# A transformer layer with FP4 feed-forward on one core: separate scale buffers for the last tiles, and some layernorm and rotary work moved from VectorE to ScalarE and GpSimd

## The chip, the cores and the metric

The kernel runs on one core of a Trainium2 chip. The metric is the device time of one execution in microseconds (us); the time of a kernel is the median of its runs. The engines are named as in the profile: PE is TensorE (matrix products; PEld its weight loads), DVE is VectorE, ACT is ScalarE, POOL is GpSimd, SP is SyncE, which issues the transfers (SPq is its queue).

## The reference

The input x is 2 sequences of 2048 tokens with 256 features. The layer is, cut to what matters:

```python
def reference(x, Wq, bq, Wk, bk, Wv, bv, Wo, bo, w_gate, w_up, w_down):
    x = x + attention(layernorm(x))      # 16 heads of 16, causal softmax
    x = x + ffn(layernorm(x))
    return x

def layernorm(x, eps=1e-5):
    m, v = mean(x, -1), var(x, -1)
    return (x - m) / sqrt(v + eps)

def rope(Y):                             # on q and k, per head
    Y2 = concat([-Y[..., 8:], Y[..., :8]], -1)
    return Y * cos + Y2 * sin

def fp4_quant_dequant(x):                # blocks of 16 along the last axis
    scale = maximum(max(abs(x)) / 6, 1e-12)
    return nearest_fp4(x / scale) * scale

def fp4_linear(x, w):
    return fp4_quant_dequant(x) @ fp4_quant_dequant(w).T

def ffn(x):                              # 256 -> 704 -> 256
    h = silu(fp4_linear(x, w_gate)) * fp4_linear(x, w_up)
    return fp4_linear(h, w_down)
```

## The kernel before

**Tiling.** A chunk is 512 tokens of one sequence; there are eight, (0,0) to (0,3) and (1,0) to (1,3), in this order. A tile is 128 tokens; a chunk has four. The heads are handled in four groups of four for each chunk, which makes 32 slots.

**A chunk's way.** `norm_steps` loads the four tiles of x, takes mean and variance (`deviation`: two DVE instructions, lines 515 and 516, then two on POOL, lines 520 and 521, that leave 1/sqrt(v+eps) in `rstd`), normalizes in place (`normed`, DVE, line 530), and turns the tile with PE (line 739), with a copy by ACT (line 745). `project_steps` makes q and k for half of the heads (`blk` 0 or 1; `i` is 0 for q and 1 for k): the product `pj` (PE, line 808), the biased copy `qb` (ACT, line 821), the product with the cosines into `t1` (DVE, line 828, from the PSUM result and the bias), the swapped halves in `t2` (DVE shuffle, line 854), times the sines (POOL, line 860), the sum into `t1` (POOL, line 863), a rounded copy `high` (ACT, line 886) and the rest `low` (POOL, line 890). High and low parts go to DRAM (SP, line 900) and come back laid out for the heads (lines 911 and 924). The first half chunk of all, called `early`, goes another way, without DRAM. In the trace the tile names of t1 and t2 are cut to "t", and "cs" is the table of cosines and sines.

For each slot, a maxima stage (`max_steps`: scores on PE, line 1064, row maxima on DVE, line 1088) precedes a value stage (`value_steps`: scores again, lines 1196 and 1204, the exponential on ACT, line 1219, and the product with the values, line 1252). The feed-forward part (`ffn_steps`) takes a tile through the attention's output product (line 1488), the first residual (line 1502), a second layernorm, `fp4` rounding (lines 554 to 593), the gate and up products (line 1543), tanh and products (1569, 1572, 1577), another `fp4` over 704 columns, and the down product (line 1636) with the second residual (line 1645). The four tiles of the last chunk (`last`) keep their data in buffers of the attention, which are free by then; they are called "own" in the trace. The bias `bob` is added to their x0 on POOL (line 1472).

`fp4` makes a small tile of scales and one of their inverses with DVE (lines 554, 557 and 558), nudges the inverse on POOL (562), multiplies by it (565), finds the rounding step on DVE (581 and 584), adds and subtracts it (587 and 590) and multiplies by the scale (593). The four large operations are POOL's, except for the 704 columns of the last chunk's tiles, where DVE has them. The weights go through `fp4` too, in the first part of the run; PE turns them (line 656). The small tiles come from rings of two buffers, called sc16 (16 blocks, for the 256 columns) and sc44 (44 blocks, for the 704 columns), for all tiles alike.

**What sets the order.** All work is handed to a planner (`Plan`) as tasks with an engine, an estimated cost, what they read and write, and a due number. The planner simulates the engines, always takes the task that can start first, and among tasks that can start within 0.03 us of each other the one with the lowest due number. The order that it finds is each engine's program order. Four of its rules matter here:

- A buffer of a ring is given to the tasks in the order in which they were added, which is that of the due numbers of their steps; only the PSUM banks `ps` are given in any order.
- A task whose due number is more than AHEAD = 3 above the lowest one that is still open isn't considered.
- PE prefers tasks of the tiling it is in (whole array, score strips, value strips): another tiling counts as CHANGE = 0.07 later in the due number.
- Due numbers are counted in units of which the 32 slots and the tail take 81 (`place`; `end` is 80). The tiles of the next to last chunk, (1,2), are spread until 4 units behind the end, so that the last of them is left for the tail, beside the last chunk's tiles. The last chunk's steps start at 80.97 with small distances.

Of the kernel before, what the change touches and what calls it, by code (L numbers as in the profile page):

```python
# [68 lines left out]
CHANGE = 0.07  # L69
# [4 lines left out]
ISSUE = 0.46  # L74

# [18 lines left out]
ROOM.update(x0=1, xT=1, x1=2, xn=2, h=1, hrT=1, step=1, fdev=2, sc16=2, sc44=2)  # L94
# [34 lines left out]
class Plan:  # L129
# [3 lines left out]
    def __init__(self):  # L133
        self.tasks = []
        self.made = {}

# [40 lines left out]
    def ordered(self):  # L177
# [33 lines left out]
        while len(out) < len(self.tasks):  # L211
            while dues and dues[-1][1] in done:
                dues.pop()
            horizon = dues[-1][0] + AHEAD
# [84 lines left out]
def landing(kb):  # L299
    return 2.0 + kb / 250  # L300
# [3 lines left out]
def layer_kernel(  # L304
# [199 lines left out]
    def deviation(pool, kind, src, thing, due):  # L504

        got = []
        dev = Thing(kind)

        def stats():
            bufs = ROOM[kind]  # L510
            st = pool.tile([P, 6], F32, tag="stats", name="stats", bufs=bufs)
            got.append(pool.tile([P, 2], F32, tag="mv", name="mv", bufs=bufs))
            got.append(pool.tile([P, 1], F32, tag="ve", name="ve", bufs=bufs))
            got.append(pool.tile([P, 1], F32, tag="rstd", name="rstd", bufs=bufs))
            nc.vector.bn_stats(st, src())
            nc.vector.bn_aggr(got[0], st)

        def power():
            mv, ve, rstd = got
            nc.gpsimd.tensor_scalar(ve, mv[:, 1:2], LN_EPS, 1.0, ALU.add, ALU.mult)  # L520
            nc.gpsimd.tensor_tensor(rstd, ve, minus_half, ALU.pow)

        add(DVE, 0.55, stats, [thing], [dev], due)
        add(POOL, 0.8, power, [dev, fixed], [dev], due)
        return got, dev

    def normed(dst, src, got, things, due):
        def run():
            mv, _, rstd = got
            nc.vector.tensor_scalar(dst(), src(), mv[:, 0:1], rstd, ALU.subtract, ALU.mult)  # L530

        add(DVE, 0.33, run, *things, due)

    def fp4(src, thing, r, n, engine=POOL, step_of=None):
# [3 lines left out]
        small16 = Thing("sc16" if nb <= 16 else "sc44")  # L538
# [10 lines left out]
        def scaled(due):  # L549
            def sizes():  # L550
                scale = ffn.tile([P, nb], F32, tag=f"scale{n}", name="scale")[:r]
                inv = ffn.tile([P, nb], F32, tag=f"inv{n}", name="inv")[:r]
                st["scale"], st["inv"] = scale, inv
                nc.vector.tensor_reduce(  # L554
                    scale, blocks(src()), AX.X, ALU.max, apply_absolute_value=True
                )
                nc.vector.tensor_scalar(scale, scale, 1.0 / 6.0, 1e-12, ALU.mult, ALU.max)
                nc.vector.reciprocal(inv, scale)  # L558
# [143 lines left out]
    def norm_steps(b, c):  # L702
# [22 lines left out]
        def stats(i, due):  # L725
            st[i]["by"] = deviation(pre, "dev", lambda: st[i]["x"], st[i]["in"], due)

        def norm(i, due):
            own = st[i]
            got, dev = own["by"]  # L730
            normed(lambda: own["x"], lambda: own["x"], got, ([dev], [own["in"]]), due)
# [27 lines left out]
    def project_steps(b, c, blk):  # L759
# [31 lines left out]
        def product_of(i, due):  # L791
# [31 lines left out]
            def cosines():  # L823
                if early and i:
                    got["t1"] = room(i, "t1")
                else:
                    got["t1"] = pre.tile([P, CH], F32, tag="t1", name="t1")
                nc.vector.scalar_tensor_tensor(
                    got["t1"], got["pj"], bias, angles[b, c][:, 0, :], ALU.add, ALU.mult
                )  # L830
# [7 lines left out]
            add(DVE, 0.67, cosines, [ps, cs_[b, c], bias_], [t1], due)  # L838
# [584 lines left out]
    def ffn_steps(b, c, i, last=False):  # L1423
# [33 lines left out]
        def load(due):  # L1457
# [4 lines left out]
            add(SP, landing(128), run, [rows_[b, c]] if last else [], [things["x0"]], due)  # L1462
# [46 lines left out]
        def scaled(due):  # L1509
# [9 lines left out]
            def step_of():  # L1519
# [5 lines left out]
                lambda: st["xn"], things["xn"], P, E, step_of=step_of if last else None  # L1525
# [68 lines left out]
        def scaled_gated(due):  # L1594
            def step_of():
# [10 lines left out]
                step_of if last else None,  # L1606
            )
# [256 lines left out]
    for at, step in sorted(begun + main + side, key=lambda x: x[0]):  # L1864
        step(at)
    for t in plan.ordered():
# [64 lines left out]
```

## Time and profile before

| What | Value |
|---|---|
| median of 3 runs | 1390.26 us (1388.22 to 1392.69) |
| profiled execution, its own time | 1384.36 us |
| its span, first to last instruction | 1382.6 us |
| PE busy | 1307.6 us, 95% |
| DVE busy | 1106.0 us, 80% |
| ACT busy | 752.0 us, 54% |
| POOL busy | 538.4 us, 39% |
| mean granted clock of TensorE | 0.972 |

The profile is a page of one execution. A row of 40 digits cuts the span into 40 equal slices and gives the busy share of each in tenths; PEclk is the clock that TensorE was granted, in tenths of full speed. A row of the timeline has the start, the duration, the engine, the line of the kernel, the operation, what it writes and reads with its shape, and in brackets how long the engine had been idle before it and what ended that. The table by stage gives busy time per engine for a stretch of the span. Matmul ends are modelled, so that a PE that is busy all the time is not PE at its peak.

### The profile page before, as it was taken

What the parts mean: (1) busy time and instruction counts of PE and PEld (TensorE: products, weight loads), DVE (VectorE), ACT (ScalarE), POOL (GpSimd) and SP (SyncE); (2) the same over time, 40 slices, a digit from 0 to 9 for tenths busy, and PEclk for the clock granted to TensorE, in tenths of its full rate; (3) what the DMA queues carried; (4) which work ended last, traced back from release to release, by engine and by line L of the source; (5) the groups of instructions that cost most, each with busy time, mean ns of one, the idle gap of its engine ahead of it and who ended that gap; (6) DMA issues with size and microseconds to landing.
All of it is one profiled execution on the core that took longest, in us unless ns stands there. A gap on an engine that the chain in (4) does not pass through costs nothing.

```text
span 1382.6 us, 27442 instructions
## 1 busy us (share of the span) xinstructions
PE 1307.6 (95%) x10269; PEld 650.5 (47%) x10269; DVE 1106.0 (80%) x2415; ACT 752.0 (54%) x1670; POOL 538.4 (39%) x685
## 2 busy tenths in 40 slices
PE   6887999999999999999988999999999999999967
PEld 4444444444544444444454555454454444444445
DVE  7788989978889988875467978997879888884286
ACT  3532665556556566558643455455655566668711
POOL 4654735434323434314345544343443232311262
PEclk9976999999999999999999999999999999999989
DMA  2544433411221401211444414240130130000000
GB/s 88 132 130 103 100 89 66 102 35 55 56 46 39 109 22 35 67 32 51 98 107 108 104 30 107 65 97 18 55 82 20 43 81 9 9 6 5 13 9 19
DMA packets 61886, 84.37 MB, mean 61 GB/s; under 512 B 14772, under 2 KB 30520, under 8 KB 61752
## 3 DMA queue, kind: packets, MB, share of 16 engines
q1 hardware_dynamic: 61744, 82.61, 23.7%
q8 instruction: 81, 1.33, 0.4%
q14 instruction: 53, 0.43, 0.1%
q10 hardware_dynamic: 8, 0.00, 0.0%
HBM read 55.09 MB, written 27.49 MB: 60 GB/s over the span
## 4 chain that ended last, share of the span: by engine, by line
PE 62%; DVE 20%; POOL 5%; issue 5%; DMA 5%; ACT 2%; SPq 0%; POOLq 0%; DVEq 0%; ACTq 0%
PE av L1252 14%; DVE parts L1088 9%; PE sc L1064 9%; PE pg L1543 9%; PE sx L1196 8%; PE sx L1204 7%; PE pd L1636 5%; PE pj L808 3%; PE pth L1403 2%; PE po L1488 1%; PE pv L990 1%; DVE scale L554 1%; PE sc L1033 1%; DVE step L581 1%; DVE step L584 1%
## 5 line engine op out<-in xcount | busy, mean ns | idle before, releaser
L1219 ACT ACTIVATE ex<-sx 128x512 f32<-128x512 f32 (+3 forms) x1280 | 593.5, 538 | 345.8 <-PE sx L1204 207.9
L1088 DVE TENSOR_REDUCE parts<-sc 128x1 f32<-128x512 f32 (+3 forms) x1152 | 638.4, 611 | 64.8 <-PE sc L1064 49.2
L1204 PE MATMUL sx<-qT,kT 64*128 64x512 f32 (+3 forms) x1280 | 337.7, 523 | 0.0
L1064 PE MATMUL sc<-kT,qT 64*128 64x512 f32 (+3 forms) x1280 | 290.3, 432 | 12.5 <-DMA kT<-parts 4.2
L1252 PE MATMUL av<-ex,v 128*32 128x512 f32 (+3 forms) x2560 | 300.1, 541 | 0.0
L1196 PE MATMUL sx<-mT,less 64*128 64x512 bf16 (+3 forms) x1280 | 250.7, 356 | 9.3 <-DVE parts L1088 3.4
L1064 PEld LDWEIGHTS sc<-kT,qT 64*128 64x128 f32 x1280 | 139.1, 192 | 176.4 <-DVE parts L1088 55.2
L1196 PEld LDWEIGHTS <-less 64*128 64x128 bf16 x1280 | 68.5, 94 | 212.9 <-issue 205.4
L562 POOL TENSOR_SCALAR inv<-inv 128x16 f32<-128x16 f32 (+2 forms) x82 | 17.7, 216 | 384.8 <-DVE inv L558 362.9
L1204 PEld LDWEIGHTS sx<-qT,kT 64*128 64x128 f32 x1280 | 132.5, 196 | 13.0 <-issue 10.6
L1636 PE MATMUL pd<-wdT,hrT 128*128 128x256 f32 (+1 forms) x384 | 100.9, 402 | 2.0 <-ACT hrT L1407 1.4
L1252 PEld LDWEIGHTS av<-ex,v 128*32 128x32 f32 x2560 | 51.7, 108 | 69.8 <-issue 59.8
L860 POOL TENSOR_TENSOR t<-t,cs 128x512 f32<-128x512 f32 x31 | 39.9, 1287 | 106.7 <-DVE t L854 100.4
L1636 PEld LDWEIGHTS pd<-wdT,hrT 128*128 128x128 f32 (+1 forms) x384 | 68.1, 191 | 27.2 <-issue 13.6
L1088 DVE TENSOR_REDUCE mx<-sc 128x1 f32<-128x128 f32 (+3 forms) x128 | 54.6, 478 | 31.2 <-PE sc L1033 31.0
L808 PE MATMUL pj<-xnT,wqkT 128*128 128x512 f32 x128 | 75.3, 685 | 3.3 <-DVE v L999 1.7
L1543 PE MATMUL pg<-wgT,xT 128*128 128x352 f32 x224 | 77.3, 477 | 0.3 <-ACT xT L1407 0.2
L1543 PE MATMUL pg<-wuT,xT 128*128 128x352 f32 x224 | 74.5, 472 | 0.2
L1033 PE MATMUL sc<-pick,mask_q 64*128 64x64 bf16 x1024 | 71.8, 202 | 0.0
L587 POOL TENSOR_TENSOR h<-h,step 128x704 f32<-128x704 f32 x28 | 47.2, 1685 | 57.8 <-DVE step L584 54.5
L1033 PE MATMUL sx<-pick,mask_k 64*128 64x64 bf16 x1024 | 63.5, 197 | 0.0
L1569 ACT ACTIVATE h<-pg 128x352 f32<-128x352 f32 x64 | 29.9, 467 | 56.8 <-PE pg L1543 51.6
(156 smaller groups left out, 1522.3 us busy)
## 6 DMA issues: line engine op xcount, KB each, us to landing
qT<-parts SPq DMA_DIRECT2D x120, 128.0 KB
kT<-parts SPq DMA_DIRECT2D x120, 128.0 KB
parts<-high SPq DMA_DIRECT2D x30, 256.0 KB
parts<-t SPq DMA_DIRECT2D x30, 256.0 KB
sums<-avs SPq DMA_DIRECT2D x28, 256.0 KB
cs<-in_rope_dram SPq DMA_DIRECT2D x8, 512.0 KB
xin<-in_L_attn_x_dram SPq DMA_DIRECT2D x28, 128.0 KB
y<-sums SPq DMA_DIRECT2D x28, 128.0 KB
```

The source lines that it names most:

```text
L587: queue.tensor_tensor(src(), src(), st["step"], ALU.add)
L808: nc.tensor.matmul(got["pj"], lhsT=wqkT[:, k, i, cols], rhs=xnTs[b, c][:, k, :], start=(k == 0), stop=(k == KE - 1),)
L860: (nc.gpsimd if early and i == 0 else queue).tensor_tensor(swapped, swapped, angles[b, c][:, 1, :], ALU.mult)
L1033: nc.tensor.matmul(sc[h][:, col + at : col + at + STRIP], lhsT=strips(mask, h, half), rhs=strips(pick, h), start=False, stop=(half == 1),)
L1064: nc.tensor.matmul(sc[h][:, :cols], lhsT=strips(qT, h, d, slice(i * P, (i + 1) * P)), rhs=strips(kT, h, duo, slice(0, cols)), start=True, ...
L1088: nc.vector.tensor_reduce(dst, got[0][h][:, :cols], AX.X, ALU.max)
L1196: nc.tensor.matmul(sc[h][:, off:], lhsT=strips(less[d], h), rhs=strips(mT, h, slice(off, CH)), start=True, stop=False,)
L1204: nc.tensor.matmul(sc[h][:, off:], lhsT=strips(kT, h, duo, slice(jj, jj + P)), rhs=strips(qT, h, d, slice(off, CH)), start=False, stop=(j ...
L1219: nc.scalar.activation(st[j, d][:, h, off:], got[0][h][:, off:], AF.Exp, scale=HD**-0.5)
L1252: nc.tensor.matmul(st["av"][SLOT * s : SLOT * (s + 1), off:], lhsT=v[:, at : at + SLOT], rhs=st[j, d][:, h, off:], start=(j == 0), stop=(j ...
L1543: nc.tensor.matmul(got[half], lhsT=split("xrT")[:, k, :], rhs=wT[:, k, half * IH : (half + 1) * IH], start=(k == 0), stop=(k == KE - 1),)
L1636: nc.tensor.matmul(st["pd"], lhsT=st["hrT"][:n, k, :], rhs=wdT[:n, k, :], start=(k == 0), stop=(k == KI - 1),)
```

## The change

Five things are changed.

1. `deviation` and `normed` get `soon`, true for the chunks (0,0), (0,1) and (0,2) in `norm_steps`. POOL then makes a third small value, shift = -mean * rstd, and the layernorm is applied by ACT as rstd * x + shift, instead of by DVE.
2. For the same chunks, without the early half of (0,0), the cosines are multiplied by POOL, from the biased copy `qb`, instead of by DVE from the PSUM result.
3. The last chunk's tiles get rings of their own for the small scale tiles (endsc16 and endsc44, two buffers each).
4. The load of x0 for the last chunk's tiles no longer waits for the attention's rows, and its due number is 1.0 lower.
5. In the planner, CHANGE goes from 0.07 to 0.1, and once the lowest open due number has come to 72 (end - NEAR), tasks up to 50 units ahead are considered instead of 3.

```diff
-CHANGE = 0.07
+CHANGE = 0.1
...
+NEAR = 8.0
+
+SOON = ((0, 0), (0, 1), (0, 2))
+COS = SOON
...
+ROOM.update(..., sc16=2, sc44=2, endsc16=2, endsc44=2)
...
-            horizon = dues[-1][0] + AHEAD
+            horizon = dues[-1][0] + (AHEAD if dues[-1][0] < self.near_end else 50.0)
...
-    def deviation(pool, kind, src, thing, due):
+    def deviation(pool, kind, src, thing, due, soon=False):
...
+            if soon:
+                nc.gpsimd.tensor_scalar(shift, mv[:, 0:1], rstd, -1.0, ALU.mult, ALU.mult)
...
-        add(POOL, 0.8, power, [dev, fixed], [dev], due)
+        add(POOL, 0.8 + 0.22 * soon, power, [dev, fixed], [dev], due)
...
-    def normed(dst, src, got, things, due):
+    def normed(dst, src, got, things, due, soon=False):
...
+            if soon:
+                nc.scalar.activation(dst(), src(), AF.Identity, bias=shift, scale=rstd)
+            else:
+                nc.vector.tensor_scalar(
+                    dst(), src(), mv[:, 0:1], rstd, ALU.subtract, ALU.mult
+                )
...
+        if soon:
+            add(ACT, on_scalar(E), run, *things, due)
+        else:
+            add(DVE, 0.33, run, *things, due)
...
-    def fp4(src, thing, r, n, engine=POOL, step_of=None):
+    def fp4(src, thing, r, n, engine=POOL, step_of=None, end=False):
...
-        small16 = Thing("sc16" if nb <= 16 else "sc44")
+        own = "end" if end else ""
+        small16 = Thing(f"{own}sc16" if nb <= 16 else f"{own}sc44")
...
+                scale = ffn.tile([P, nb], F32, tag=f"{own}scale{n}", name="scale")[:r]
+                inv = ffn.tile([P, nb], F32, tag=f"{own}inv{n}", name="inv")[:r]
...
+                if early or (b, c) not in COS:
+                    nc.vector.scalar_tensor_tensor(
+                        got["t1"], got["pj"], bias, angles[b, c][:, 0, :], ALU.add, ALU.mult
+                    )
+                else:
+                    nc.gpsimd.tensor_tensor(
+                        got["t1"], got["qb"], angles[b, c][:, 0, :], ALU.mult
+                    )
...
-            add(DVE, 0.67, cosines, [ps, cs_[b, c], bias_], [t1], due)
+            if early or (b, c) not in COS:
+                add(DVE, 0.67, cosines, [ps, cs_[b, c], bias_], [t1], due)
+            else:
+                add(POOL, on_pool(CH), cosines, [qb, cs_[b, c]], [t1], due)
...
-            add(SP, landing(128), run, [rows_[b, c]] if last else [], [things["x0"]], due)
+            add(SP, landing(128), run, [], [things["x0"]], due - 1.0 * last)
...
+    plan.near_end = end - NEAR
```

In `ffn_steps`, both calls of `fp4` pass `last` as `end`.

## The prediction

> **What bounds the kernel now.** I read the page first, then the table by stage, then the timelines of the two places where TensorE (PE) is not full.
>
> The page, its head and its slices of 34.6 us:
>
> ```profile
> span 1382.6 us, 27442 instructions
> PE 1307.6 (95%) x10269; PEld 650.5 (47%) x10269; DVE 1106.0 (80%) x2415; ACT 752.0 (54%) x1670; POOL 538.4 (39%) x685
> ...
> PE   6887999999999999999988999999999999999967
> ...
> DVE  7788989978889988875467978997879888884286
> ...
> PEclk9976999999999999999999999999999999999989
> ```
>
> PE is full but for the first four slices and the last two; only there can an unburdened DVE pay directly. The stages, columns as named, busy us and instruction counts:
>
> ```profile
> core 0: us, PE busy (x) PEld busy (x) DVE busy (x) ACT busy (x) POOL busy (x), PEclk, DMA share, GB/s
> 200.00:1250.00 1050.00, 1025.05 (x8182) 498.45 (x8176) 871.95 (x1861) 602.17 (x1317) 391.75 (x455) 1.00 0.23 59
> ...
> 1264.00:1312.00 48.00, 47.30 (x418) 19.77 (x415) 9.24 (x18) 37.20 (x86) 7.08 (x7) 1.00 0.01 4
> 1312.00:1326.00 14.00, 4.65 (x23) 3.44 (x20) 9.82 (x29) 1.14 (x5) 11.03 (x22) 0.75 0.13 39
> 1326.00:1366.00 40.00, 37.72 (x142) 24.68 (x142) 35.86 (x70) 8.86 (x24) 15.25 (x23) 0.96 0.02 7
> ```
>
> In the last softmax stage (1264 to 1312) DVE and POOL lie idle. Then attention ends, PE stands, and DVE and POOL carry the last tiles' chain. From 1326 DVE is the full one (35.86 of 40). The timeline shows what waits there; "x" and "xn" belong to the last tile of chunk (1,2), "own" to the four tiles of chunk (1,3):
>
> ```profile
> 1292.69 1.77 DVE L530 TENSOR_SCALAR xn<-x,mv,rstd 128x256 f32<-128x256 f32 x1 [1.64 <-POOL rstd L521]
> ...
> 1310.10 0.42 DVE L1645 TENSOR_TENSOR x<-pd,x 128x256 f32<-128x256 f32 x1 [15.64 <-PE pd L1636]
> ...
> 1317.38 0.42 DVE L554 TENSOR_REDUCE scale<-own 128x16 f32<-128x256 f32 x1
> ...
> 1318.22 0.36 DVE L554 TENSOR_REDUCE scale<-xn 128x16 f32<-128x256 f32 x1
> ...
> 1325.11 0.69 PE L1403 MATMUL pth<-ident,own 128*128 128x128 f32 x2 [9.14 <-POOL own L593]
> ```
>
> Tile xn is normalized at 1294.46, and its scale, which needs nothing else, comes 23.8 us later, behind the first own tile's, though DVE stood idle for 15.64. The code says why: the sc16 buffers are handed out in the order of the due numbers, and xn's scale has 81.37, between own tile 0 (81.25) and own tile 1 (81.42). For sc44 it is 83.16, behind own tiles 0, 1 and 2.
>
> The early part, waits from 0 to 140 us (total, times, longest):
>
> ```profile
> POOL t L860 <- DVE t L854: 13.0, 4, 6.9
> ...
> PE ptr L656 <- POOL wr L593: 7.5, 3, 4.4
> ```
>
> POOL waits for DVE's shuffles, but PE also waits for POOL's rounded weights: both of these engines are on the path in turn.
>
> **The change part by part.** Sums are against the profiled execution: 1384.36 us, that is its span of 1382.6 and 1.76 around it. The median of the three runs shown is 1390.26, 5.9 higher; I carry the difference over to the median.
>
> *Start, 0 to 24 us.* Four norms of 0.41 (L530 first) leave DVE for ACT, and POOL gets four `shift` operations. A POOL operation of this size has a pitch of 0.28 (ve at 5.69, rstd at 5.97), and POOL works without a break there from 5.69: at most 4 x 0.28 = 1.1 lost. At least 0: the chain runs through the transfer of Wq until 9.03, and the first projection starts at 12.30. ACT has 1.5 of 4 us free in 8 to 12; an ACT operation over 128x256 takes 0.38 (L745), as long as what it replaces. I take +0.5, between the ends.
>
> *Layernorm and cosines, 24 to 200 us.* Eight L530 (0.32 to 0.81, together 3.96) and ten L828 (0.74 each, 7.4) leave DVE. Two of the L828 lie behind 200 us, where PE is full; of the others all but the L530 at 59.60 and the L828 at 63.63 lie where DVE is at 2.9 to 4.0 of 4 us: 0.75+0.32+0.75+0.40+0.46 (33 to 50 us), 0.74+0.74 (85 and 101), 0.74+3x0.40+0.81+0.75+0.74 (130 to 192), sum 8.4. That is the most it can gain. POOL gets ten multiplies of 1.28 (row L860: 1287 ns) and eight shifts at 0.28. The multiply precedes the sines in POOL's queue and needs qb from ACT, as the shuffle does. Where the shuffle is late (POOL idle 4.67 before the L860 at 35.68, 6.87 at 87.38, 2.76 at 175.86, 11.62 at 195.59) it is hidden, and costs 1.28 if DVE shuffles at once. Where POOL works without a break on the chain (49.3 and 103.3) it costs 2 x 1.28 = 2.6; where the shuffle comes at once (66.00), 1.28 - 0.73 = 0.55. Behind POOL wait ACT's rounding (L886), the low part, and SP's stores of the parts; SP issues in order, so the key loads and weight loads behind them shift too. The shifts delay each norm, and so the transposes, by 0.28: four on the path, 1.1.
>
> More POOL work also holds DVE up: the tiny mask-slot operations (L1126, L1129: medians 0.18 and 0.19) last up to 1.7 beside POOL, and their means are 0.11 above the median at a POOL share of 39%. So 12.8 us more of POOL in 176 (7%) cost some 100 such operations 100 x 0.11 x 7/39 = 2.0. Loss bound: 2.6+0.55+1.1+2.0 = 6.2. I take half of the gain (half, because DVE and POOL alternate on the chain) less the 2.6 that are in sight: 8.4/2 - 2.6, about -2; the rest of the loss stays in the ends, -8 and +6.
>
> The Trainium skill speaks against this move: "SBUF — State Buffer", section "Who interferes with whom", says that a VectorE instruction in a two-port mode, or with two SBUF inputs, and a GpSimd instruction that reads SBUF exclude each other for the whole instruction. Row: L530 took 1.77 at 1292.69 beside a POOL add of 1.69, where its median is 0.41. By the rule at its worst all ten multiplies would hold DVE for their whole length, 12.8 us, and the early part would end at +11 instead of -2; the measured means above say 2.0.
>
> *CHANGE from 0.07 to 0.1.* PE is kept in one tiling a little longer. From 200 to 1310 us I count 1032 changes of tiling in the timeline. One costs 0.09: score pairs follow each other at 0.46 (1285.77, 1286.23), a value group after 0.55 (1286.78). Five in a hundred fewer would be 52 x 0.09 = 4.6 gained; fed in larger lumps, DVE's maxima would wait longer for scores, and 5% of L1088's 64.8 us idle is 3.2 lost. Neither is shown; -1, ends -4.6 and +3.2.
>
> *The end.* (a) The four x0 loads no longer wait for the attention rows: issued at 1311.02, they let POOL's bias add start at 1313.23 and the first add on DVE at 1313.99. Its products began at 1312.28 and a like group takes 1.13, so 0.6 is won; and four bias adds (2.85 us of POOL) leave 1313 to 1317. SP has only two stores around them. The last load needs a buffer that the last score frees, at about 1306; it is not late. (b) With scales apart, and the limit of look-ahead lifted once 8 plan units are left (the loop has 81 over some 1312 us, so about the last 130), xn's scale and rounding go to 1294 to 1301, where DVE and POOL idle. Its transposes cost PE 0.4 in a full stretch. On POOL they stood between own tile 0's steps (0.62 at 1319.66, 0.72 at 1322.11): -1.3. (c) xn's gate and up products, 16 matmuls of 1.35 us per four, 5.4, fit into PE's 9.14 idle. Then their four DVE steps (4 x 0.51) and the scaling of h (0.88+0.18+0.43+0.52+0.53 = 2.5) leave the stretch where DVE is full, for one with 4.2 idle: up to -4.5. (d) xn's down product (4.48 from 1370.65) stands before the last own tile's transposes (1375.06), whose input was there at 1372.98: up to -2.1. Sum 0.6+1.3+4.5+2.1 = 8.5, and 1.5 more if the clock stays up (eight gate matmuls took 4.05 at 1326, 2.53 at 1330). Some of it overlaps, and own tiles still need their latency: I take -6, ends -10 and -1 (only the load).
>
> Sum: +0.5 - 2 - 1 - 6 = -8.5: 1375.9 for a profiled run, **1381.8** for the median.
>
> **The rivals.**
> *Clock regained* (faster still). PE ran at a clock of 0.50 in 28 to 32, 76 to 88 and 112 to 136, each after a gap (PE 1.32 of 4 us at 108). Summed over the 4 us slices from 24 to 140, 29 us of clock are missing. If an earlier DVE closes the gap before 112, the 13.6 of the last stretch go; but DVE is at 3.9 of 4 there, so I count 8: 1373.8. Against: that gap ended on POOL's rounded weights.
> *POOL takes over the early path* (slower). PE's wait for the rounded weights (4.4 at its longest, before the half-clock stretch) ends with POOL. If nearly all ten multiplies stand in such chains, 12.8 + 1.1 + 2.0 are lost and 4.2 + 6 + 1 gained, +5 with the start: 1396. It decides from some eight of ten on the path; I see two or three.
> *Tail given back* (no change). PE is full from 1264 to 1312, and ACT has 37.20 of 48: if xn's products slip in there, attention ends as much later, 5.4 of the 6 are gone, and with the early part at zero: 1389.
>
> **How the numbers follow.** Forecast 0.53, clock regained 0.17, tail given back 0.13, POOL takes over 0.17. The first two are faster: 0.70; 0.13 the same; 0.17 slower. 0.3% is 4.2 us, about what a measurement here tells apart. Forecast alone: 1376 to 1387. The range for 8 in 10 takes in the clock case with some of its early bound (1368) and the slower case (1396).
>
> **What would show it.** L530 on xin and first gone from DVE, an ACT operation of about 0.38 in their place, 12 of them; ten POOL multiplies of 1.28 writing t, 21 L828 rows of t instead of 31; POOL about 15 us busier, DVE 11 to 13 less. xn's scale before 1302 and before own's; PE's wait for the first own transposes cut from 9.1 to under 5; from the last value group to the end about 68 us instead of 74. DVE idle before L860 smaller. Wrong it would be if early slices stay at a low clock for longer, if POOL is what PE and SP wait for before 200 us, or if 200 to 1250 moves by more than 5 us through the order alone.

## The result and the profile after

| | before | after |
|---|---|---|
| median of 20 runs each | 1389.74 us (1387.15 to 1393.28) | 1393.86 us (1388.78 to 1398.31) |
| profiled execution, its span | 1384.36, 1382.6 | 1393.44, 1391.6 |

The ratio is 1.0031, 95% interval 1.0021 to 1.0040: the change makes the kernel about 4.3 us slower, where 8.5 us faster was forecast.

Page of the kernel after: its head and the row of the clock, in slices of 34.8 us.

```profile
span 1391.6 us, 27474 instructions
...
PE 1318.3 (95%) x10269; PEld 656.6 (47%) x10269; DVE 1105.9 (79%) x2393; ACT 755.3 (54%) x1682; POOL 552.8 (40%) x707
...
PEclk8877999999999999999999999999999999999998
```

POOL has 14.4 us more, as expected. DVE's total is the same although 22 of its instructions are gone: before 200 us its work fell from 162 to 148 us (the table by stage of both kernels, 0 to 200 us), and its other instructions took longer later (no_early below, with all of before's DVE instructions, has 1114.6).

Two stretches of the table by stage, first before, then after. The columns are those of the prediction (from and to, length, busy us and count of each engine, clock, DMA):

```profile
24.00:200.00 176.00, 154.99 (x1305) 81.75 (x1306) 145.16 (x367) 84.25 (x205) 95.90 (x142) 0.84 0.42 104
200.00:1310.00 1110.00, 1085.05 (x8703) 523.42 (x8695) 890.05 (x1896) 648.66 (x1420) 401.60 (x466) 1.00 0.22 56
...
24.00:200.00 176.00, 152.67 (x1268) 79.42 (x1269) 134.00 (x342) 83.10 (x203) 103.47 (x155) 0.84 0.44 102
200.00:1310.00 1110.00, 1087.50 (x8648) 525.99 (x8646) 903.35 (x1912) 645.84 (x1412) 412.33 (x478) 0.99 0.23 56
```

The early clock digits, 8877 after 9976, look lower, but the mean clock from 24 to 200 us is 0.84 in both, and the digits change from one execution to the next (8886 in only_tail and 8977 in tail_skip below, whose early part has before's order). The middle is as full of PE as before.

These profiles hold more than the change. PE's idle time, its span less its busy time, is 75.0 us before and 73.3 after. The 9.0 us between the two spans are PE's busy time, which is 10.7 us longer for the same 10269 matmuls: PE ran slower. Read in windows of 10 us from 200 to 1300 us, what the granted clock lacks to full speed adds up to 3.4 us in before and to 11.9 in after. And before's profiled execution is a good one, 5.4 us under its median, where after's is 0.4 under.

The end of the kernel after, in the stretches that lie as far behind ACT's last copy of a slot's result (1317.33 us; 1308.52 before) as 1312 to 1326 and 1326 to 1366 did before:

```profile
1320.80:1334.80 14.00, 10.41 (x43) 7.36 (x42) 11.18 (x33) 2.40 (x7) 7.89 (x18) 0.95 0.01 2
1334.80:1374.80 40.00, 34.35 (x129) 22.28 (x128) 35.77 (x59) 7.90 (x21) 15.92 (x19) 0.93 0.02 7
```

PE's hole behind attention's end is smaller (10.41 us busy of 14, 4.65 before). DVE is still the full engine behind it (35.77 of 40, 35.86 before), with about as much of POOL beside it (15.92, 15.25 before).

Each kernel's slots can be laid side by side by ACT's copy of a slot's result (`avs`), which ends the slot. This table, worked out from the timelines, has the time of that copy in before and the differences to it, in us:

| slot | before | after | only_soon | only_cos | only_change | only_tail |
|---|---|---|---|---|---|---|
| 0 | 53.4 | +3.1 | +5.3 | -1.0 | +1.0 | +0.4 |
| 3 | 107.3 | +8.1 | +7.9 | +7.8 | +1.2 | +0.3 |
| 6 | 219.9 | +8.0 | +19.6 | +11.6 | +0.7 | +1.0 |
| 10 | 406.3 | +10.5 | +15.2 | +5.4 | -0.6 | +1.3 |
| 31 | 1308.5 | +8.8 | +15.5 | +8.5 | -0.7 | +3.7 |

The whole change is behind by 3 us at slot 0 and by 8 at slot 3. Later the difference goes from +0.8 (slot 7) to +15.4 (slot 11), since the place of a slot among the other work is the planner's too, and ends at +8.8. From the last copy to the end are 74.1 us before and 74.3 after.

One profile is one execution. Up to slot 23 only_tail has before's order on PE and still differs from it by up to 1.3 us; at slot 24, still in the same order, it steps to 3.4. That step is the clock: from 950 to 960 us it is 0.66 in only_tail and 1.00 in before. Five kernels below were built to keep before's order on PE up to the tail, and their drift from slot 6 to slot 31 follows what their clock lacks, from 200 to 1300 us, beyond the 3.4 us of before: +2.7 for 3.4 us in only_tail, +2.0 for 3.4 in tail_skip, +1.4 for 1.7 in soon_old, +4.3 for 5.1 in soon_old12, +2.0 for 1.7 in cos_old. So the first slots are read below, and late differences of this size are not.

### The profile page after: what moved, and what is told of

Read it like the earlier page. It is cut to its first block, busy times and chain, and to the rows that moved or that the text cites. A ratio compares the mean times of both kernels' runs of the same rounds, so it can differ in the third digit from the quotient of the medians.

```text
span 1391.6 us, 27474 instructions
## 1 busy us (share of the span) xinstructions
PE 1318.3 (95%) x10269; PEld 656.6 (47%) x10269; DVE 1105.9 (79%) x2393; ACT 755.3 (54%) x1682; POOL 552.8 (40%) x707
## 4 chain that ended last, share of the span: by engine, by line
PE 61%; DVE 21%; issue 6%; DMA 4%; POOL 3%; ACT 2%; SPq 2%; POOLq 0%; DVEq 0%; ACTq 0%
PE av L1288 14%; DVE parts L1124 9%; PE pg L1580 9%; PE sc L1100 9%; PE sx L1232 8%; PE sx L1240 7%; PE pd L1674 5%; PE pj L836 2%; PE pth L1439 2%; PE po L1524 2%; DVE scale L573 1%; DVE step L600 1%; PE sc L1069 1%; PE pv L1026 1%; DVE step L603 1%
## 5 line engine op out<-in xcount | busy, mean ns | idle before, releaser
L1240 PEld LDWEIGHTS sx<-qT,kT 64*128 64x128 f32 x1280 | 133.2, 198 | 11.6 <-issue 9.3
L836 PE MATMUL pj<-xnT,wqkT 128*128 128x512 f32 x128 | 73.1, 668 | 3.5 <-DVE v L1035 1.8
L527 POOL TENSOR_SCALAR ve<-mv 128x1 f32<-128x1 f32 x64 | 12.6, 197 | 137.7 <-DVE mv L523 134.5
```

Source lines behind the costliest of these rows:

```text
L836: nc.tensor.matmul(got["pj"], lhsT=wqkT[:, k, i, cols], rhs=xnTs[b, c][:, k, :], start=(k == 0), stop=(k == KE - 1),)
L1240: nc.tensor.matmul(sc[h][:, off:], lhsT=strips(kT, h, duo, slice(jj, jj + P)), rhs=strips(qT, h, d, slice(off, CH)), start=False, stop=(j ...
```

## The experiments

Two theories stood first. *Work*: the moved operations are too dear on ACT and POOL, as in the rival "POOL takes over". *Order*: the planner, given other costs and engines, finds another order for the in-order queues, and that order is worse. First each part alone; CHANGE is 0.07 except where named.

**The end alone.** Kept: scales apart, the loads, the longer look-ahead.

```diff
-CHANGE = 0.1
+CHANGE = 0.07
-SOON = ((0, 0), (0, 1), (0, 2))
-COS = SOON
+SOON = ()
+COS = ()
```

> The kernel before with the end's parts alone: rings of their own for the last tiles' scales, the earlier x0 load, and the look-ahead opened for the last 8 plan units; the order of the first nine tenths of PE's program is unchanged. My prediction's theory: 6 us faster (ratio 0.996), the stretch from the last copy of av to the end 68 us instead of 74.1. Rival, read from the changed kernel's trace (the stretch is 74.3 there, DVE is busy 54.7 us in it instead of 53.8): the work moved forward frees PE and POOL but not DVE, whose own instructions are held up longer by POOL's rounding of the left-over tile; then 0 to 2 us either way and a stretch of 73 to 75.

Measured: 1387.70 us, ratio 0.9984 (0.9972 to 0.9996): 2.2 us won.

**Layernorm alone** (`SOON` kept, the rest off).

> The kernel before with the layernorm of the first three chunks applied by ACT alone. My prediction's theory: DVE's 5.9 us less in a full stretch is worth 1 to 3 us (ratio 0.998 to 0.999). Rival A (POOL on the path): the extra 0.28 us on POOL and the later start cost 0 to 2 us more (1.000 to 1.001). Rival B (the order): the whole plan behind it is shuffled, and the time moves by up to 5 us with no link to DVE's 5.9 us; then the growth lies behind 200 us.

Measured: 1403.24 us, ratio 1.0096 (1.0073 to 1.0118).

**Cosines alone** (`COS` kept, the rest off).

> The kernel before with the cosines of the first three chunks multiplied by POOL alone. My prediction's theory: 1 us faster to 1 us slower (DVE's 7.4 us against 2.6 us on POOL's chain). Rival A (POOL on the path): the multiplies stand before the sines in POOL's queue and the keys come later; 5 to 8 us slower (ratio 1.004 to 1.006), all of it by the fifth value stage, some 160 us in. Rival B (the order): any sign, the difference behind 200 us.

Measured: 1394.06 us, ratio 1.0033 (1.0020 to 1.0046).

**CHANGE alone** (0.1, the rest off).

> The kernel before with CHANGE at 0.1 alone. My prediction's theory: 1 us faster, within 4.6 faster and 3.2 slower. Rival (the order costs it): 4 us or more slower (ratio 1.003 or more), which would by itself be the whole loss of the changed kernel; the changes of tiling from 200 to 1310 us fewer than 1032 all the same.

Measured: 1385.99 us, ratio 0.9973 (0.9955 to 0.9991).

The parts alone add up to +0.86%, the whole has +0.31%, so they don't simply add. The layernorm alone costs three times what the whole change does, the cosines alone as much.

**Work without order, order without work.** The planner sees and books an operation apart from what is then issued, so the two can be parted. In soon_old and cos_old the operations run on ACT and POOL, but are planned as before, so that every queue keeps its old order. In soon_plan and cos_plan the planner is told of the move and finds the new order, but the operations stay on DVE. (In cos_plan the multiply reads `qb` instead of the PSUM result.)

```diff
 # soon_old: booked as DVE's, issued on ACT
-        add(POOL, 0.8 + 0.22 * soon, power, [dev, fixed], [dev], due)
+        add(POOL, 0.8, power, [dev, fixed], [dev], due)
...
-        if soon:
-            add(ACT, on_scalar(E), run, *things, due)
-        else:
-            add(DVE, 0.33, run, *things, due)
+        add(DVE, 0.33, run, *things, due)
 # soon_plan: booked as ACT's, issued on DVE
-            if soon:
+            if False:
                 nc.scalar.activation(dst(), src(), AF.Identity, bias=shift, scale=rstd)
 # cos_plan: booked as POOL's, issued on DVE
-                    nc.gpsimd.tensor_tensor(
+                    nc.vector.tensor_tensor(
                         got["t1"], got["qb"], angles[b, c][:, 0, :], ALU.mult
```

In cos_old, DVE's multiply is left out for these chunks and POOL's multiply stands behind DVE's shuffle, ahead of the sines.

> The layernorm of the first three chunks on ACT (with POOL's shift), but the planner is told the costs and the engine of before, so that all other instructions keep the order of before. Theory 'the work itself' (the start measured 2.8 us late with the layernorm on ACT: first projection at 13.80 and first DVE product at 17.22, before 12.30 and 14.40): the start is late here too, the first value stage ends 3 to 6 us later, and most of the 13 us of the part alone remains (ratio 1.005 to 1.010). Theory 'the order': most of it goes (ratio 0.998 to 1.002), and stays in the kernel that has the new order without the new work.

> The order that the planner finds with the layernorm on ACT, but the layernorm is computed by DVE as before, at the place that the plan gave it, without the shift. Theory 'the order': 8 to 13 us slower (ratio 1.006 to 1.010). Theory 'the work itself': within 3 us of before (0.998 to 1.002).

> The cosines of the first three chunks multiplied by POOL right ahead of the sines, but the plan of before, so that all else keeps its order. Theory 'POOL on the path': each of the multiplies delays the sines by up to 1.28 us; the fourth value stage ends 4 to 8 us later, ratio 1.002 to 1.005. Theory 'the order': within 2 us of before or faster (0.997 to 1.001), since DVE has 7.4 us less.

> The order that the planner finds with the cosines on POOL, but the product is made by DVE, from qb, at the place that the plan gave it. Theory 'the order': the fourth value stage ends some 8 us later as with the part alone (7.8), ratio 1.002 to 1.005; the low part's store again stands behind a weight load in SP's queue. Theory 'POOL on the path': within 2 us of before.

| | work and order | work, old order | order, old work |
|---|---|---|---|
| layernorm | 1.0096 | 1.0017 (1.0003 to 1.0031) | 1.0093 (1.0074 to 1.0111) |
| cosines | 1.0033 | 0.9997 (0.9985 to 1.0010) | 1.0082 (1.0061 to 1.0103) |

This is the main finding. The order alone loses as much as the part, or more. When the queues keep their order, the move of the ten multiplies costs nothing that can be measured, what POOL gets and what DVE is spared taken together. *Work* falls for the cosines, and keeps a small rest, 2.4 us, for the layernorm. The right column is not the order in itself: there DVE does work that the plan has on another engine, and in cos_plan its multiply reads `qb`. The next two runs have no such difference.

**Orders with no work moved.** The four parts are off, and one number of the planner is a little different, the booked cost of DVE's cosine multiply:

```diff
-                add(DVE, 0.67, cosines, [ps, cs_[b, c], bias_], [t1], due)
+                add(DVE, 0.69, cosines, [ps, cs_[b, c], bias_], [t1], due)
```

> All four parts of the change are off. One number of the planner alone is different: it books 0.69 instead of 0.67 for DVE's cosine multiply, so the same instructions stand in another order. Theory 'the loss is in the order of the in-order queues, not in the moved work': the time moves by more than its interval though nothing was moved, in either direction, by something like the sizes seen for the reordered kernels (0.3 to 1 %, 4 to 13 us), and the shift is there by the third chunk's slots (before 220 us). Rival 'the order is harmless, the loss needs the moved work': within 0.2 % of before (1.000 +- 0.002).

Measured: 1407.1 us, ratio 1.0123 (1.0101 to 1.0144). No instruction was added or moved to another engine, and it is the slowest of all. It stands at +2.9 at slot 3, +14.0 at slot 6 and +23.8 at slot 31, so it loses in the middle too.

> All four parts off; the planner books 0.65 instead of 0.67 for DVE's cosine multiply. A second draw of an order with no work moved. Theory 'an order near this one is drawn from a spread of some 1 %, and before is one of its better draws': slower, by 0.2 to 1.2 %. Rival 'only a longer booking delays the keys, a shorter one helps or does nothing': 0.997 to 1.002.

With 0.65: 1391.91 us, ratio 1.0033 (1.0020 to 1.0046). Its slots are within 0.5 us of before up to slot 9; +3.4 comes at slot 10 and +6.5 by slot 28. Both of these orders are slower than that of before; two others below, with CHANGE at 0.08 and 0.1, are faster. A few draws don't make a distribution, but they show that two orders which the planner takes for nearly equal can differ by over 1%. Of placebo4's late steps 5.1 us are again what the clock lacks beyond before's, so its loss is read from the medians alone.

**Idle or clock.** The kernels that lose, lose in two ways. only_cos has 81.3 us of idle PE (75.0 before), at the mean granted clock that before's runs have (0.968 in both). placebo3 has 80.1, and a lower clock as well: its four runs have 0.960 or 0.961, which none of the 116 runs of before beside the experiments has (0.963 to 0.974, mean 0.968). By an estimate, 0.008 of 1400 us are 11 us, more than half of its 17. The 20 runs of the whole change have a mean of 0.965, and 0.003 of 1390 us are about 4, the size of its loss, while in the profiles its PE is idle no longer than before's. The estimate takes PE as always busy. So part of what an order costs comes as a lower clock; what makes it fall was not tested, and no run parts it from the waits.

**What in the order costs.** In the kernel with the cosines alone, one stretch stands out. Its row in the table by stage:

```profile
72.00:84.00 12.00, 6.55 (x44) 3.81 (x45) 6.41 (x20) 0.00 (x0) 1.92 (x5) 0.65 0.30 85
```

Its timeline, with lines of SP, DVE and PE in order of time (start, duration, engine, line, operation; in brackets the idle time before and what ended it):

```profile
73.67 0.56 SPq L1353 DMA_DIRECT2D over<-sums  x1
74.33 0.39 SPq L664 DMA_DIRECT2D wr<-in_L_ffn_w_up_dram  x1
...
77.57 0.42 DVE L573 TENSOR_REDUCE scale<-wr 128x16 f32<-128x256 f32 x1 [2.32 <-DMA wr<-in_L_ffn_w_up_dram]
...
78.40 3.07 DVE L1124 TENSOR_REDUCE mx<-sc 128x1 f32<-128x128 f32 x10
...
78.69 0.58 PE L1100 MATMUL sc<-kT,qT 64*128 64x256 f32 x1 [3.00 <-DVE mx L1124]
```

SP's queue has `over<-sums`, which waits for an earlier store, ahead of the load of the up weights. The load is late, DVE stands at its scale for 2.32 us, ten maxima whose scores are ready stand behind that scale in DVE's queue, and PE waits 3.00 us for the maxima to free its scores' banks. PE is busy 6.55 of 12 us (9.52 before). Before, the same load went out at 68.65, ahead of `over<-sums` at 72.42.

Two kernels turn single pairs of SP's queue round in that order, and nothing else:

```diff
+MOVES = (("load", 27, 28), ("sums", 35, 36))
...
+    ordered = plan.ordered()
+    for name, n, m in MOVES:
+        at = [i for i, t in enumerate(ordered) if t.engine == SP][n]
+        to = [i for i, t in enumerate(ordered) if t.engine == SP][m]
+        ordered.insert(to, ordered.pop(at))
-    for t in plan.ordered():
+    for t in ordered:
```

sp_swap has the first pair alone (the load of the gate weights ahead of the store of chunk 1's key parts), sp_swap2 both.

> The kernel with the cosines alone on GpSimd (only_cos, 1.0033, third slot at +7.8), in its own order on every engine but for one pair on SP: the weight load that stood ahead of the key parts' store of chunk 1 is issued after it. Theory 'SP's queue, in which the load waits for its buffer, holds the keys up': the store goes out at about 55 us instead of 58.5, and the third slot and those behind it come 2 to 4 us earlier; ratio about 1.001. Rival 'the keys are late anyway, or the load then is': third slot unchanged within 1 us, ratio 1.003.

Measured: 1393.97 us, ratio 1.0037 (1.0020 to 1.0054), slot 3 at +7.6. The store did go out at 54.81 instead of 58.51, but the key loads, behind other entries of the queue, at 60.80 instead of 60.45. The suspicion was wrong for this pair.

> As the kernel before, and a second pair of SP turned round: the up weights' load of the same stretch is issued before the sums' load that waits for a store to land. Theory 'DVE and PE idle in 72 to 84 us because the weights come late': the load goes out at about 69 instead of 74.3 us, PE's busy time in 72 to 84 rises from 6.55 towards 9.5, third slot 5 to 8 us earlier than in only_cos, ratio about 1.000. Rival 'DVE waits for other work there': PE's busy time in the window within 1 us of 6.55, ratio as with one pair.

Measured: 1389.67 us, ratio 1.0000 (0.9988 to 1.0012). The same row of the table by stage for sp_swap2, and its timeline:

```profile
72.00:84.00 12.00, 10.33 (x64) 5.46 (x64) 8.04 (x23) 0.69 (x1) 2.39 (x5) 0.57 0.29 84
```

```profile
70.01 0.33 SPq L665 DMA_DIRECT2D wr<-in_L_ffn_w_up_dram  x1
72.99 0.55 SPq L1354 DMA_DIRECT2D over<-sums  x1
...
74.50 0.40 DVE L574 TENSOR_REDUCE scale<-wr 128x16 f32<-128x256 f32 x1
...
75.31 3.07 DVE L1125 TENSOR_REDUCE mx<-sc 128x1 f32<-128x128 f32 x10
```

The scale waits for nothing, the maxima start 3.1 us earlier, PE has 10.33 of 12 us, and slot 3 stands at +4.8 instead of +7.8. With the first pair alone worth nothing, it is this one load, issued 4.3 us earlier, that takes back the 0.33% that the cosines' part cost. The second pair was not turned round alone. In the trace 3.0 of the 7.8 us at slot 3 come back; the other 4.8 stay there, though the time is that of before, so a difference at one slot is not yet one in the time.

**The same in the whole change?** There both of these loads precede `over<-sums`. The place that looked alike is later: chunk 2's key loads stood behind a store of sums and a weight load, and went out at 106.25.

```diff
+MOVES = (("sums", 49, 51), ("load", 49, 51))
```

> The whole change, in its own order but for SP at one place: the store of the value sums and the up weights' load that stood ahead of chunk 2's key loads (105.83 us, each waiting for its own data) are issued after them. Theory 'SP's queue is where the new order loses': the key loads go out at 103 to 104 instead of 106.25 us, the fourth slot comes 2 to 3 us earlier than at 166.7, ratio about 1.001 (1.0031 without). Rival 'the keys' parts land no earlier': loads within 0.7 us of 106.25 and ratio 1.003.

Measured: 1392.16 us, ratio 1.0027 (1.0012 to 1.0041). The key loads did start at 100.79, 5.5 us earlier, and slot 4 came at 167.2 instead of 166.7. So these entries are not what the whole change loses by. That it is the order there too is worked out from the parts: in the old order their work costs 0.17% and nothing that can be measured, inside the whole they cost 0.73% (no_early below). Which entries of which queue cost the 4.5 us between slots 2 and 3 stays open.

**The rest of the layernorm.** soon_old once more, with the moved layernorm left out for the first chunk:

```diff
-SOON = ((0, 0), (0, 1), (0, 2))
+SOON = ((0, 1), (0, 2))
```

> The order of before, and layernorm by ScalarE for the second and third chunk alone, not for the first, whose chain starts the program. Theory 'what the moved layernorm itself costs is the start': slot 0 within 0.7 us of before (it was +3.0 with all three chunks), ratio 0.999 to 1.0005 (1.0017 with all three). Rival 'ACT's slower layernorm costs in every chunk': slot 0 at 0, but +1 to +2 by slot 2 and +1 to +3 at the end, ratio 1.001 or more.

Measured: 1391.59 us, ratio 1.0005 (0.9988 to 1.0023). Slot 0 stands at -0.7 and slots 1 to 3 within 0.2 us of before, against +3.0 and +4.3 at slots 0 and 3 in soon_old. So the cost is at the start, by the slots. The medians point the same way, but their intervals overlap, and this profile drifts to +5.2 by slot 31, with the clock as said above.

The start of the kernel after, in the timeline:

```profile
11.99 0.60 ACT L541 ACTIVATE first<-first,shift,rstd 128x256 f32<-128x256 f32 x1
...
13.55 3.70 PE L836 MATMUL pj<-xnT,wqkT 128*128 128x512 f32 x8 [0.46 <-ACT xnT L773]
```

And the groups of the moved operations in the kernel after (count; busy us, mean ns; idle before):

```profile
L541 ACT ACTIVATE xin<-xin,shift,rstd 128x256 f32<-128x256 f32 x8 | 4.9, 617 | 5.9 <-POOL shift L531 5.9
...
L861 POOL TENSOR_TENSOR t<-qb,cs 128x512 f32<-128x512 f32 x10 | 12.7, 1273 | 15.5 <-ACT qb L849 15.4
```

ACT's layernorm takes 0.60 to 0.62 us. The fourth one ends the chain, and the first projection starts at 13.55 instead of 12.30. Its shift was there at 10.72; ACT began it at 11.99, behind two copies of its own queue, of which one waited for PE.

**The end.** What steps (b) to (d) of the prediction became, in the timeline of the kernel after:

```profile
1304.21 0.42 DVE L573 TENSOR_REDUCE scale<-xn 128x16 f32<-128x256 f32 x1
...
1320.13 1.45 PE L1580 MATMUL pg<-wgT,xT 128*128 128x352 f32 x4 [0.46 <-ACT xT L1443]
...
1322.46 3.72 PE L1524 MATMUL po<-woT,own 128*128 128x256 f32 x16
...
1332.80 0.44 PE L1439 MATMUL pth<-ident,own 128*128 128x128 f32 x2 [3.07 <-POOL own L612]
1333.75 4.07 PE L1580 MATMUL pg<-wgT,own 128*128 128x352 f32 x8 [0.52 <-ACT own L1443]
...
1381.40 1.54 PE L1439 MATMUL pth<-ident,h 128*128 128x128 f32 x6 [3.37 <-DVE h L612]
1383.19 5.31 PE L1674 MATMUL pd<-wdT,hrT 128*128 128x256 f32 x12 [0.25 <-ACT hrT L1443]
```

The left-over tile's scale is ahead of attention's end, its gate and up products lie in PE's old hole, and PE's wait is 3.07 instead of 9.14, all as written. But own tiles' output products start 5.1 us behind the last copy instead of 3.8, since the left-over tile's work stands ahead; eight gate matmuls still take 4.07; and at the very end PE idles 3.37 us and then runs the last product in 5.31 us. Before, it had done the left-over tile's down product at that place, and the last one took 3.05:

```profile
1370.65 4.48 PE L1636 MATMUL pd<-wdT,hrT 128*128 128x256 f32 x12 [0.46 <-ACT hrT L1407]
1375.06 0.88 PE L1403 MATMUL pth<-ident,h 128*128 128x128 f32 x6
1376.39 3.05 PE L1636 MATMUL pd<-wdT,hrT 128*128 128x256 f32 x12 [0.46 <-ACT hrT L1407]
```

And DVE is held up. In only_tail's timeline, POOL's large steps on the left-over tile's h now fall beside DVE's own:

```profile
1341.14 2.32 POOL L609 TENSOR_TENSOR h<-h,step 128x704 f32<-128x704 f32 x1
1341.97 1.88 DVE L600 TENSOR_SCALAR step<-h 128x704 int32<-128x704 int32 x1
...
1344.41 1.66 POOL L612 TENSOR_TENSOR h<-h,scale 128x704 f32<-128x704 f32 x1
1344.86 1.96 DVE L606 TENSOR_TENSOR h<-h,step 128x704 f32<-128x704 f32 x1
```

Undisturbed, as for the last own tile in the same kernel, these two DVE steps take 0.53 and 0.89 us. The test leaves POOL's four large steps on that tile's h out of only_tail:

```diff
             def added():
+                if skip:
+                    return
                 queue.tensor_tensor(src(), src(), st["step"], ALU.add)
...
```

> The end of the change alone (compare with only_tail), where GpSimd's rounding of the left-over tile's h is left out (its additions, subtractions and scalings, four 128x704 instructions: this tile's output is not rounded as it should be, and the time is that of the rest). Theory 'after attention, DVE's own rounding of h is held up by GpSimd's, which now falls beside it, by about 5 us': the stretch from the last value stage's copy to the end falls by 3 to 5 us against only_tail's 73.1, and DVE's L600 and L606 go from 1.9 back to under 1.0. Rival 'DVE's later steps bound it through their own chain': the stretch falls by less than 1 us.

Measured: 1384.99 us, ratio 0.9966 (0.9952 to 0.9981) against only_tail's 0.9984. The same two steps in tail_skip's timeline:

```profile
1341.59 0.93 DVE L602 TENSOR_SCALAR step<-h 128x704 int32<-128x704 int32 x1
...
1343.42 0.89 DVE L610 TENSOR_TENSOR h<-h,step 128x704 f32<-128x704 f32 x1
```

From the last copy to the end are 70.1 us instead of 73.1; the two steps shown have 2.0 of these 3. So POOL's rounding, most of it by falling beside DVE's, cost about 3 us of what the end was to bring. The medians, 2.7 us apart, point the same way, but their intervals overlap.

**End and CHANGE together**, the early parts off:

> The end of the change (scales apart, loads, longer look-ahead) and CHANGE 0.1 together, layernorm and cosines as before. If what the two gave alone adds up (0.9984 and 0.9973), 0.9957: 1384 us, with the early milestones within 1.5 us of before and the value stages from slot 7 on 1 to 3 us earlier. Rival 'parts don't add, since each reorders the other's queue': anything from 0.996 to 1.003, with the difference already present in the first eight slots.

Measured: 1384.63 us, ratio 0.9958 (0.9944 to 0.9972), just the sum of the two. This version beats both kernels. It also says what the early parts cost inside the whole change: 1.0031 / 0.9958 = 1.0073, or 10.2 us.

**A warm end.** The same with four extra matmuls, whose results are overwritten, ahead of the last transposes of h:

```diff
...
+            if warm:
+                for _ in range(warm):
+                    nc.tensor.matmul(
+                        got[0].rearrange("p k o -> p (k o)"),
+                        lhsT=ident,
+                        rhs=wdT[:, :2, :].rearrange("p k o -> p (k o)"),
+                        start=True,
+                        stop=True,
+                    )
```

> The kernel with the end and CHANGE 0.1, and four extra matmuls, whose result is overwritten at once, ahead of the last own tile's transposes of h, in the gap in which PE idles for DVE. Theory 'the left-over tile's down product was PE's cover, and without it the last transposes and the down product run at half clock': the last pth at 0.9 instead of 1.5 and the last pd at about 3.1 instead of 5.4 us, the time 2 to 3 us (0.2 %) under the kernel without them. Rival 'the gap, not the work in it, costs': the extra matmuls only delay, 0 to +1.5 us.

Measured: 1383.97 us, ratio 0.9956 (0.9939 to 0.9973). In its timeline the last product is fast:

```profile
1368.29 3.70 PE L1440 MATMUL pth<-wdT,ident 128*128 128x512 f32 x8
1371.83 0.82 PE L1449 MATMUL pth<-ident,h 128*128 128x128 f32 x6
1373.10 3.05 PE L1685 MATMUL pd<-wdT,hrT 128*128 128x256 f32 x12 [0.46 <-ACT hrT L1453]
```

It took 4.73 in no_early. From DVE's last step on h to the end are 7.6 us instead of 9.3. The mechanism is shown in the trace; a gain of 1.6 us in the time can't be told from none with these intervals.

**Is CHANGE's gain one of fewer changes of tiling?** CHANGE at 0.08, the rest off:

> All four parts off; CHANGE at 0.08. If CHANGE wins by fewer changes of tiling on PE (1018 with 0.1 against 1032 with 0.07, between 200 and 1310 us), a third of the way wins a third: 0.9991, some 5 changes fewer. Rival 'CHANGE 0.1 was one lucky order': anything in 0.997 to 1.010, with no relation to the number of changes.

Measured: 1387.04 us, ratio 0.9985 (0.9974 to 0.9996). Between 200 and 1310 us, with each row of the timeline counted once, there are 986 changes of tiling in before (the prediction counted 1032), 981 with 0.08, 976 with 0.1. At the prediction's 0.09 each, 5 and 10 fewer are worth 0.5 and 0.9 us, less than the measured 2.1 and 3.8; placebo3 has 979, and is the slowest. So fewer changes alone don't explain the gain. Whether it is CHANGE's or that of two good orders stays open.

## Why the prediction was wrong, point by point

The step that failed is *Layernorm and cosines, 24 to 200 us*, with its "about -2" between -8 and +6. With the start it was to be -1.5; inside the whole change the two measured +10.2. Everything else was forecast at -7 and measured -5.8 (no_early).

- **The gain of the early part was no gain.** DVE did lose the work (11.2 us less between 24 and 200, of which the prediction put 8.4 in slices where DVE was full), but slot 3 came 8 us later. DVE at 3.9 of 4 us was read as the limit. In cos_old it has ten multiplies less in the old order, and the time is the same: relief of DVE, with POOL's extra work beside it, was worth nothing. That DVE, POOL, PE and SP wait for each other in a ring there is the likely reason; it is read from the waits, not shown.
- **The loss was bounded from the wrong rows.** The step priced POOL's own time, 2.6 + 0.55 + 1.1 + 2.0. cos_old measures that for the cosines, less what DVE is spared, at nothing. What it named in passing and put no price on, that SP issues in order and that the loads behind shift too, is what cost in only_cos: one load 4.3 us late was worth 0.33%. The step took the order of before for given and moved the operations in it, while the planner redraws the whole order. Rows of the old order can't bound that. placebo3 shows how much it can be: +17 us with no work moved. Which entries cost it in the whole change stays open, and so does how much of it is the lower clock.
- **Start +0.5 (0 to 1.1).** +1.25 at the first projection and +3.1 at slot 0, so outside its ends. The layernorm on ACT was priced at 0.38, the row of a copy out of PSUM (L745); from SBUF with a scale and a bias for each partition it takes 0.60. And the `shift` holds more than itself: DVE's statistics of the next tiles wait for it (0.57 and 0.78 us in the trace), and the last layernorm waits in ACT's queue.
- **CHANGE -1 (-4.6 to +3.2).** -3.8 alone; inside the ends, but by luck: the price per change of tiling gives 0.9, and the rest is not explained.
- **End -6 (-10 to -1).** -2.2. (a) The bias adds did go ahead of attention's end, but the first own residual in only_tail comes 6.3 us behind the last copy, 5.5 before: it now waits for PE's later output product, so the 0.6 is gone. (b) and (c) were right in what moves where; (c)'s 4.5 was mis-sized, as POOL's part of the moved steps fell beside DVE's and took about 3 back. (d) has the wrong sign: the left-over product that was "in the way" was what kept PE busy and at full clock, as tail_warm's trace agrees, and the end behind DVE's last step is 0.8 us longer (9.6 before, 10.4 in only_tail), not 2.1 shorter.
- **The Trainium skill's rule** of "SBUF — State Buffer", section "Who interferes with whom", was weighed for the early part, with +12.8 us at its worst. Nothing like that is in the time of cos_old (0.9997). Some of it may be in the engine: DVE's total fell by 2.3 us there, though 7.3 us of multiplies were gone, so its other operations took some 5 us longer. At the end, where the prediction did not apply the rule, the rows agree with it: 1.88 for 0.53 us beside POOL.
- **What was to show it.** Twelve layernorms on ACT, ten multiplies on POOL, 14.4 us more for POOL and a wait of 3.07 are there as written. DVE's 11 to 13 us less are not in its total, and from the last copy to the end it is 74.3 us, not some six less. The middle as a whole did not move by more than 5 us (+8.0 at slot 6, +9.5 at slot 30), though single slots did.
- **The rivals.** "POOL takes over" named nearly the right time (1396) and the right place by luck, and not the cause: POOL's multiplies didn't cost, the queues' order did. "Clock regained" did not happen: the clock from 24 to 200 us is 0.84 in both, and it fell later, in the middle. "Tail given back" did not happen: the gate and up products ran behind attention's end, from 1320.13 on, not in it.

Chances of 0.17 for slower were too low, because the order, the one thing that all four parts change at once, was no rival; it stands only as a sign in the prediction's last sentence.

## What to carry to other kernels

Where a planner writes the order of in-order queues from estimated costs, any change of a cost is also a new order of everything, and that alone moved this kernel by 0.3 to 1.2%. Part the two: run the new work in the old order and the old work in the new order, before believing a gain or a loss. When a slow order is found, look first for a load that stands in a queue behind an entry that waits; one such load, turned round, took back a whole part's loss here, while other entries that looked alike gave nothing. Compare the profiled execution with its median, and the clock with the idle time, before a difference is read from one pair of profiles. And at the tail, work that seems in the way of the last chain may be what keeps PE's clock up (1.6 us in the trace here, not to be told from none in the time).

## What the runs showed of the hardware

- An activation over 128x256 from SBUF to SBUF with scale and bias from SBUF takes 0.60 us on ACT, a copy of the same size out of PSUM 0.37.
- After the same 3.37 us of PE idle, the last six transposes took 1.54 us in after, only_tail and tail_skip, and 0.87 in no_early, where the product behind them took 4.73 instead of 5.00 to 5.38: the step down of the clock falls at different moments. The Trainium skill, "TensorE: Matmul & The Clock Gate", Part 1, says that the gate works by a free-running window of about 3.4 us, and that the moment varies with where in the window the work lands; these rows agree.
- The clock falls in the middle of a full stretch as well. In after it is 0.50 from 272 to 278 us, behind four us (266 to 270) in which PE was busy for 2.95, and the output product's four matmuls at 273.62 take 2.07 us; four of them took 1.13 in before, at 1288.79.
- Part of the spread between executions of one kernel goes with the clock. In no_early's runs, the mean granted clock of 0.972 goes with spans of 1377.5 and 1380.0 us, 0.963 with 1387.4.
